# Half of the query turns and half of the context turns as two-byte DMA transposes in a two-layer transformer kernel

## The chip, the cores and the metric

The kernel runs on one core of a Trainium2 chip. The core has five engines, each with an instruction queue of its own that is worked off in order: TensorE (matrix products, named PE in the profile; PEld is its weight load), VectorE (DVE), ScalarE (ACT), GpSimd (POOL) and SyncE (SP), which only issues DMAs. Sixteen DMA engines move the data of all queues. The metric is the device time of one execution in microseconds. Before the change it is 1984.88 us, the median of three runs (1981.24 to 1986.15).

## The reference

Two layers work on x of shape (4, 512, 512): four sequences of 512 tokens with 512 features. Each layer adds an attention and a mixture of experts to x, both taken from the same layer norm. The change lies in the attention of the first layer, which in short is

```python
xn = layernorm(x)
q  = rope(rmsnorm(xn @ Wq))              # 16 heads of 128
lk = rope(rmsnorm(xn @ Wlk)); lv = xn @ Wlv
# a compressed memory: every 4 tokens make one entry, keys ck and values cv
sc = q @ ck.T * scale                    # causal, the 8 largest per query are kept
ctx_sparse = softmax(top8(sc)) @ cv
# a local window: 128 tokens back
ctx_local = softmax(mask(q @ lk.T * scale)) @ lv
out = concat_heads((ctx_sparse + ctx_local) * 0.5) @ Wo
x = x + out + moe(xn)                    # 8 experts, the 2 best per token
```

The second layer (plain attention with 16 heads of 32 and a second mixture of experts) is not touched.

## The kernel before, in words

**Steps.** The first layer's attention is a loop over 32 steps. A step is a pair (g, b): a group g of two heads (there are eight) and a sequence b (four). Step i computes the attention of its two heads, while the projections of step i+1 are computed between its parts. `project(i + 1)` returns the pieces of the next step, which the loop calls at chosen places: `first`, `second`, `third`, `fourth` and `fifth` compute queries, keys and values of 512 tokens by seven block products in place of eight (L750 to L802). The queries come out with tokens on the partitions, in two tiles `qb[0]` (tokens 0 to 255) and `qb[1]` (256 to 511).

**Turns.** The scores need queries with features on the partitions, so each half is turned: `turn_queries(t)` (L737) makes four 128x128 transposes on TensorE into one bank of PSUM (tile `trq`), and ScalarE copies the bank into `qkT` (L742). The keys are turned in the same way by `turn_keys` (L744). `qkT` has one buffer, shared by the step at work and the next.

**Attention of one head.** `scores` (L807) makes compressed scores (tile `sp`, L820) and local ones (`st`, L831); `turn` (L859) turns the chosen weights into `sT`, with two ScalarE copies; `context` (L870) multiplies by the values (L881 to L886), and ScalarE and VectorE scale and add both parts into a tile of tag `ctx` (L897, L899). This tag has two buffers. `turn_context(i, h, ...)` (L903) turns the 512x128 contexts of a head by four transposes on TensorE (tile `trc`) and a ScalarE copy into `cT` (L907), one tile with one buffer for both heads.

**Output.** In steps 5 to 23 `output7` (L932) multiplies `cT` by Wo with seven block products; its `before` part needs only the first 256 tokens of head 0 (the product x, tile `ox`, L945). In the other steps `output` (L909) makes four products over both heads (`op`, L914).

**What else lies in the steps.** `run0((i, h))` calls the jobs listed for a place of a step. From step 5 to step 22 these are the experts of the first layer, two tiles of 128 tokens per step: `apply` (L545, the products `hp_r` at L552, the sum `yr_r` at L555, its store `yd` at L561), the fetch of the weights by GpSimd (L489), and the tokens of later tiles. These tokens already come by transfer: they lie in DRAM split into low and high two-byte halves, GpSimd gathers them (L524), SyncE stores them (L529, `xrd_r`), and a DMA transpose loads them turned (L534, `xT_r`), one half-step ahead of their use. From step 24 on the expert outputs are gathered and added, and from step 29 the next layer's layer norm begins, with its stores on SyncE (L250, L1125).

**What sets the order.** The framework plans the kernel ahead of its execution: each instruction goes to its engine's queue in an order that follows the text of the program, corrected by estimated times, and waits by semaphores on what it reads or overwrites. A tile that reuses a buffer waits until all users of the buffer's last tile are done. Instructions wrapped in `tc.keep_in_program_order` keep the order of the text among each other; the rest may be moved. The DMAs of SyncE stand in one queue: `L685` loads sums of the inputs for the next step, `L1271` copies 32 rows of compressed values for a later step, L561 stores expert outputs.

Of the kernel before, what the change touches and what calls it, by code (L numbers as in the profile page):

```python
# [12 lines left out]
F32 = mybir.dt.float32  # L13
# [7 lines left out]
P = 128  # L21
# [3 lines left out]
TC = S // P  # L25
KC = HID // P
NH, D = 16, 128
# [9 lines left out]
HG = 2  # L37
# [9 lines left out]
U16 = mybir.dt.uint16  # L47
# [3 lines left out]
def two_layers(ctx: ExitStack, tc: tile.TileContext, a: dict, out: bass.AP, large: bass.AP):  # L51
# [3 lines left out]
    nc = tc.nc  # L55
    V, G, A, PE = nc.vector, nc.gpsimd, nc.scalar, nc.tensor
# [4 lines left out]
    dram = ctx.enter_context(tc.tile_pool(reuse_waits="tile", name="dram", bufs=1, space=DRAM))  # L61
# [6 lines left out]
    wk0 = layer0.enter_context(tc.tile_pool(reuse_waits="tile", name="att0", bufs=2))  # L68
# [5 lines left out]
    def psum(tag, name):  # L74
        return ps.tile([P, 512], F32, tag=tag, name=name, bufs={"mm": 3, "sc": 3, "tr": 2}[tag])
# [22 lines left out]
    def load_later(g):  # L98

        w = load_block(g, "wB")  # L100
        b2 = wpool.tile([P, 2, 3 * D], F32, tag="b2", name=f"b2_{g}")
        for i, nm in enumerate(("bA", "bB")):
            nc.sync.dma_start(out=b2[:, i, :], in_=a[nm][g].partition_broadcast(P))
        return [[None, w], b2]

    def load_out(g):
        wo = wpool.tile([P, HG, HID], F32, tag="Wo", name=f"Wo_{g}", bufs=1)
        nc.sync.dma_start(out=wo, in_=a["Wo"][ds(g * HG * D, HG * D), :].rearrange("(h p) c -> p h c", p=P))
        return wo
# [357 lines left out]
    class Experts:  # L467
# [58 lines left out]
        def store_halves(self, i):  # L526
            if i < NS:
                xd = self.xd[i] = dram.tile([P, 2, HID], U16, tag="xrd", name=f"xrd_{self.r.name}_{i}", bufs=3)
                tc.keep_in_program_order(nc.sync.dma_start(out=xd.rearrange("p h d -> p (h d)"), in_=self.x.pop(i)))  # L529
# [6 lines left out]
        def turn(self, i):  # L536
            x = self.x[i]
            tr = self.bank("tr", f"trm_{self.r.name}_{i}")
            for k in range(KC):
                PE.transpose(tr[:, ts(k, P)], x[:, ts(k, P)], ident)  # L540
            xT = self.pool.tile([P, KC, P], F32, tag="xT", name=f"xT_{self.r.name}_{i}", bufs=2 if self.silu else 1)
            A.copy(xT, tr.rearrange("p (k t) -> p k t", k=KC))
            self.x[i] = xT
# [136 lines left out]
    def load_sums(i):  # L680

        for n in range(4):
            xs[n] = wk0.tile([P, 2, 256], F32, tag=f"x{n}", name=f"x{n}_{i}", bufs=1)
            if i >= B:
                nc.sync.dma_start(out=xs[n].rearrange("p k t -> p (k t)"), in_=xsd[steps[i][1], n])  # L685

    def project(i):


# [3 lines left out]
        qkT = qp.tile([P, 2 * HG, S], F32, tag="qkT", name=f"qkT_{g}_{b}", bufs=1)  # L693
        x11, x12, x21, x22 = (xnT[:, ts(f, 2), ds(b * S + t * 256, 256)] for t in range(2) for f in range(2))
        rows3 = [P, 2, 3 * D]
        u, qb, sq = {}, {}, {}
# [40 lines left out]
        def turn_queries(t):  # L737
            tr = psum("tr", f"trq_{i}_{t}")
            for h in range(HG):
                for c in range(2):  # L740
                    PE.transpose(tr[:, ts(h * 2 + c, P)], qb[t][:, c, ts(h, D)], ident)  # L741
            A.copy(qkT[:, 0:HG, ts(t, 256)], tr.rearrange("p (h t) -> p h t", h=HG))  # L742

        def turn_keys(h):  # L744
            tr = psum("tr", f"trk_{i}_{h}")
            for t in range(TC):
                PE.transpose(tr[:, ts(t, P)], lv[:, t, 2, 0:D] if h else qb[t // 2][:, t % 2, ts(2, D)], ident)  # L747
            A.activation(qkT[:, HG + h, :], tr, AF.Copy, scale=turned[:, 0:1])
# [121 lines left out]
    def context(i, h, lT, sT, lv):  # L870

        g, b = steps[i]
        nm = f"{g}_{b}_{h}"
        U = D + 1

        ca, cb, cc = (psum("sc", f"c{x}_{nm}") for x in "abc")
        loc = [ca[:, ts(t, U)] if t < 3 else cb[:, 0:U] for t in range(TC)]
        spa = [cc[:, 0:U], cc[:, ts(1, U)], cb[:, ts(1, U)], cb[:, ts(2, U)]]
        for t in range(TC):
            if t:  # L880
                PE.matmul(loc[t], lhsT=lT[:, ds((t - 1) * 256 + P, P)], rhs=lv[:, t - 1, h, :],  # L881
                          start=True, stop=False)
            PE.matmul(loc[t], lhsT=lT[:, ds(t * 256, P)], rhs=lv[:, t, h, :],  # L883
                      start=(t == 0), stop=True)
        for t, at, n in ((2, 0, 96), (3, 1, P), (0, 0, P), (1, 2, P)):
            PE.matmul(spa[t], lhsT=sT[0:n, ts(at, P)], rhs=cv[0:n, b, :] if t else cv0s[i % 2],  # L886
                      start=True, stop=True)
        sums = small.tile([P, 8], F32, tag="sums", name=f"sums_{nm}")
        for dst, bank, n in ((0, ca, 3), (3, cb, 3), (6, cc, 2)):
            V.tensor_scalar(sums[:, ds(dst, n)],  # L890
                            bank[:, 0 : n * U].rearrange("p (n u) -> p n u", u=U)[:, :, D],
                            1e-30, None, ALU.max)
        V.reciprocal(sums, sums)
        ctx_ = wk0.tile([P, TC, D], F32, tag="ctx", name=f"ctx_{nm}")
        for t in (2, 3, 0, 1):
            at = (6, 7, 4, 5)[t]
            A.activation(ctx_[:, t, :], spa[t][:, 0:D], AF.Copy, scale=sums[:, at : at + 1])  # L897
        for t in range(TC):
            V.scalar_tensor_tensor(ctx_[:, t, :], loc[t][:, 0:D], sums[:, t : t + 1], ctx_[:, t, :],  # L899
                                   ALU.mult, ALU.add)  # L900
        return ctx_

    def turn_context(i, h, ctx_, cT):  # L903
        tr = psum("tr", f"trc_{i}_{h}")
        for t in range(TC):
            PE.transpose(tr[:, ts(t, P)], ctx_[:, t, :], ident)
        A.copy(cT[:, h, :], tr)  # L907
# [125 lines left out]
    for b in range(1, B):  # L1033
        i = b - 2
# [118 lines left out]
    for n in range(3 * TC):  # L1153
        i, t = 29 + n // TC, n % TC
# [22 lines left out]
    qkT, sums_x, first, second, third, fourth, fifth, turn_queries, turn_keys, sevenths = project(0)  # L1177
# [83 lines left out]
    for i, (g, b) in enumerate(steps):  # L1261
        if b == 0:
            if g:
                out_w[g] = load_out(g)
            if g + 1 < NH // HG:
                groups[g + 1] = load_later(g + 1)
        more = i + 1 < len(steps)
        turn_last = turn_keys
        now = qkT
        cT = qp.tile([P, HG, S], F32, tag="cT", name=f"cT_{g}_{b}", bufs=1)  # L1270
        nc.sync.dma_start(out=cv0s[i % 2][96:P, 0:D], in_=cv[0:32, b, 0:D])  # L1271
        em0, lT0 = scores(i, 0, now, (lambda: (turn_last(1), next(comp[0]))) if i == 0 else None)
        if i:
            turn_last(1)
        if more:
            load_sums(i + 1)
            qkT, sums_x, first, second, third, fourth, fifth, turn_queries, turn_keys, _ = project(i + 1)
            first()
            sums_x()
            if b == 2 and g + 1 in groups:  # L1280
                groups[g + 1][0][0] = load_block(g + 1, "wA")
        run0((i, 0))
        em1, lT1 = scores(i, 1, now)
        if i == 0:
            second(0)
        sT0 = turn(i, 0, em0)
        run0((i, 1))
        if more:
            if i:
                second(0)  # L1290
            if i != 3:
                turn_queries(0)
        ctx0 = context(i, 0, lT0, sT0, lv)
        if more:
            if i == 3:
                turn_queries(0)
            second(1)
        sT1 = turn(i, 1, em1)
        if more:
            third()  # L1300
        if b == 2 and g + 1 in groups:
            combine_weights(g + 1)
        run0((i, 2))
        ctx1 = context(i, 1, lT1, sT1, lv)
        turn_context(i, 0, ctx0, cT)
        if i == 5 or b == 0 and 5 < i < 24:
            combine_out(g)
        run0((i, 3))
        if more:
            fourth()  # L1310


            if 5 <= i < 24:
                turn_queries(1)
                turn_keys(0)
                fifth()
            else:
                fifth()
        seven = 5 <= i < 24
        if seven:  # L1320
            before, rest_ = output7(i, cT)
            before()
        turn_context(i, 1, ctx1, cT)
        if more and not 5 <= i < 24:
            turn_queries(1)
            turn_keys(0)
        run0((i, 3.5))
        if seven:
            rest_()
        else:  # L1330
            for t in range(TC):
                output(i, t, cT)
        run0((i, 4))
# [240 lines left out]
    order1, whole_, halves_ = [], list(range(FULL)), list(range(FULL, NS))  # L1574
# [875 lines left out]
```

## Time and profile before

| | us |
|---|---|
| median of three runs | 1984.88 |
| the profiled execution | 1984.9 |
| its span, first to last instruction | 1983.1 |
| a step with experts (6 to 18) | 44.0 |
| a step after the experts (24 to 28) | 38.0 |
| mean of one transpose as listed, L741 and L906 | 0.276 |
| ScalarE copy behind it, L742 and L907 | 0.587 and 0.577 |

The granted TensorE clock is 0.997 over the span. A line of the groups or of the timeline gives the line of the kernel, the engine, the operation, the tiles (written<-read) with shape and type, and the count; the timeline begins with start and length in us, both merged over the count. Matmuls are pipelined, so lengths of neighbours overlap, and the time that one takes from TensorE is read from the distance of starts. In the waits, a line names who waited, for whom, the total in us, the number of waits and the longest. In the windows each engine has its busy time and instruction count; PEclk is the granted clock, DMA the busy share of the sixteen DMA engines.

### The profile page before, as it was taken

The page shows a single profiled execution, that of the slowest core. Times are in us where ns is not written, and L with a number is a line of the kernel's source. Part 1 is how long each engine was busy: PE and PEld are TensorE (multiplying, and loading weights), DVE is VectorE, ACT ScalarE, POOL GpSimd, SP SyncE. Part 2 cuts the span into 40 slices and gives each one's busy share as a digit, 9 for nine tenths or more (in the row PEclk, how much of TensorE's full clock was granted, in tenths as well). Part 3 has the DMA queues.
Part 4 walks back from the last instruction along what each step waited for, and adds up shares of the span by engine and source line. Part 5 has one row for each costly group of instructions (what it writes and reads, how often), then busy time and mean ns, then how long its engine had stood idle before and what let it go on. Part 6 is the DMA issues. An engine that isn't in the chain of part 4 may idle for free.

```text
span 1983.1 us, 28429 instructions
## 1 busy us (share of the span) xinstructions
PE 1953.7 (99%) x9222; PEld 1228.8 (62%) x9222; DVE 1481.3 (75%) x3662; ACT 870.8 (44%) x2650; POOL 755.7 (38%) x827
## 2 busy tenths in 40 slices
PE   7999999999999999999999999999999999999998
PEld 4676667777777677776667776666434445445443
DVE  7778878777776777777678888788696655666886
ACT  5556544444444444444444455445234433333342
POOL 5422254443423333334432454455114432333551
PEclk9999999999999999999999999999999999999999
DMA  9224355544554464356572322232317775775441
GB/s 298 97 69 134 128 162 161 165 134 130 159 157 134 139 183 139 112 163 191 192 223 57 97 75 65 86 96 75 119 44 265 254 255 186 276 251 177 156 157 63
DMA packets 147294, 298.74 MB, mean 151 GB/s; under 512 B 53568, under 2 KB 67008, under 8 KB 135360
## 3 DMA queue, kind: packets, MB, share of 16 engines
q1 hardware_dynamic: 118912, 145.81, 24.0%
q0 software_dynamic: 27072, 148.91, 22.6%
q10 hardware_dynamic: 1152, 2.10, 0.3%
q8 instruction: 76, 1.25, 0.3%
q14 instruction: 82, 0.67, 0.1%
HBM read 230.44 MB, written 56.36 MB: 145 GB/s over the span
## 4 chain that ended last, share of the span: by engine, by line
PE 85%; DVE 9%; ACT 3%; issue 1%; DMA 1%; POOL 0%; SPq 0%; DVEq 0%; ACTq 0%; POOLq 0%
PE p L717 24%; PE hp_r L552 13%; PE op L914 4%; PE st L831 4%; PE st L1483 3%; PE po L1621 3%; PE cx L1497 3%; PE qp L1459 3%; PE sp L820 3%; PE ox L945 2%; PE o L1566 2%; PE ca L883 2%; PE oz L945 1%; PE trk L747 1%; PE trq L741 1%
## 5 line engine op out<-in xcount | busy, mean ns | idle before, releaser
L552 PE MATMUL hp_r<-we_r,xT_r 128*128 128x512 f32 (+1 forms) x592 | 224.2, 596 | 0.8 <-DVE qk L1472 0.8
L606 POOL TENSOR_TENSOR ss_q<-ss_q,nhalf 128x4 f32<-128x4 f32 x64 | 71.1, 1111 | 366.1 <-ACT ss_q L603 366.1
L839 POOL TENSOR_TENSOR lT<-lT,lmask 128x512 f32<-128x512 f32 (+1 forms) x128 | 150.2, 1187 | 105.8 <-ACT lT L835 104.8
L717 PE MATMUL p<-wT,x 128*128 128x384 f32 x512 | 176.6, 488 | 1.5 <-DVE wT L121 1.1
L717 PE MATMUL p<-wB,x 128*128 128x384 f32 x512 | 177.0, 490 | 0.1
L717 PE MATMUL p<-wA,xnT 128*128 128x384 f32 x512 | 173.6, 490 | 0.4 <-DVE u L757 0.3
L835 ACT ACTIVATE lT<-st,ss_k 128x256 f32<-128x256 f32 (+1 forms) x256 | 98.9, 441 | 161.1 <-PE st L831 159.4
L1485 ACT ACTIVATE pT<-st 128x1024 f32<-128x1024 f32 x128 | 123.3, 1016 | 59.0 <-PE st L1483 43.7
L552 PEld LDWEIGHTS hp_r<-we_r,xT_r 128*128 128x128 f32 (+1 forms) x592 | 83.2, 170 | 96.2 <-issue 93.4
L717 PEld LDWEIGHTS p<-wB,x 128*128 128x128 f32 x512 | 94.2, 191 | 63.1 <-issue 7.3
L717 PEld LDWEIGHTS p<-wT,x 128*128 128x128 f32 x512 | 93.4, 190 | 63.8 <-issue 4.8
L717 PEld LDWEIGHTS p<-wA,xnT 128*128 128x128 f32 x512 | 95.0, 192 | 60.4 <-DVE u L757 2.9
L601 ACT ACTIVATE sq_q<-qb 128x128 f32<-128x128 f32 x256 | 79.2, 310 | 117.1 <-DVE qb L763 54.9
L831 PE MATMUL st<-qkT 128*128 128x256 f32 (+1 forms) x512 | 114.6, 353 | 0.0
L569 POOL DMA_INDIRECT row_r<-yd,slot_r x64 | 72.1, 1127 | 75.0 <-issue 28.7
L831 PEld LDWEIGHTS st<-qkT 128*128 128x128 f32 x512 | 92.2, 190 | 11.5 <-issue 1.8
L914 PE MATMUL op<-Wo,cT 128*128 128x512 f32 x208 | 92.8, 593 | 0.0
L735 ACT ACTIVATE qb<-qb,ss_q 128x128 f32<-128x128 f32 x256 | 81.8, 392 | 21.3 <-POOL ss_k L605 16.0
L606 POOL TENSOR_TENSOR ss_k<-ss_k,nhalf 128x2 f32<-128x2 f32 (+1 forms) x96 | 86.7, 903 | 8.0
L742 ACT COPY qkT<-trq 128x512 f32<-128x512 f32 x64 | 37.6, 587 | 118.0 <-PE trq L741 78.8
L717 PE MATMUL p<-wT,xnT 128*128 128x384 f32 x256 | 88.1, 487 | 0.3 <-DVE wT L121 0.3
L605 POOL TENSOR_SCALAR ss_k<-ss_k 128x2 f32<-128x2 f32 (+1 forms) x96 | 35.0, 364 | 137.4 <-ACT sq_k L601 131.2
(388 smaller groups left out, 4598.1 us busy)
## 6 DMA issues: line engine op xcount, KB each, us to landing
x<-xsd SPq DMA_DIRECT2D x112, 256.0 KB
yd<-yr_r SPq DMA_DIRECT2D x72, 256.0 KB
xrd_r<-xr_r SPq DMA_DIRECT2D x36, 256.0 KB
wA<-in_wA SPq DMA_DIRECT2D x16, 384.0 KB
wB<-in_wB SPq DMA_DIRECT2D x16, 384.0 KB
xnd<-xn SPq DMA_DIRECT2D x24, 256.0 KB
accd<-acc SPq DMA_DIRECT2D x18, 256.0 KB
acc<-in_x SPq DMA_DIRECT2D x16, 256.0 KB
```

The costliest lines, as they stand in the source:

```text
L552: PE.matmul(hp[ts(h, m), :], lhsT=xT[:, k, ts(h, m)], rhs=w[:, ts(k, HID)], start=(k == 0), stop=(k == KC - 1))
L569: G.indirect_dma_start(out=x, out_offset=None, in_=self.yd, in_offset=at_rows(self.r.slot[:, k, n : n + 1]))
L601: pin(A.activation(sq, x[:, h, :], AF.Square, accum_out=ss[:, j : j + 1]))
L606: pin(G.tensor_tensor(ss, ss, nhalf[:, 0:n], ALU.pow))
L717: fixed(PE.matmul(p, lhsT=x[:, k, ts(c, P)], rhs=w[:, k, :], start=(k == 0), stop=(k == 1)))
L735: A.activation(x[:, j, :], x[:, j, :], AF.Copy, scale=scale[:, n : n + 1])
L820: PE.matmul(sp[:, seen[t]], lhsT=qkT[:, h, ts(t, P)], rhs=ckT[:, b, 0 : 32 * (t + 1)], start=True, stop=True)
L831: PE.matmul(st[:, ds((t % 2) * 256, n)], lhsT=qkT[:, HG + h, ts(t, P)], rhs=qkT[:, h, ds(t * P, n)], start=True, stop=True)
L835: A.activation(lT[:, ds(half * 512 + c * 256, n)], st[:, ds(c * 256, n)], AF.Exp, scale=norm_k[(i, h)][2 * half + c])
L839: G.tensor_tensor(dst, dst, lmask.rearrange("p a w j -> p (a w j)")[:, 0:n], ALU.mult)
L914: PE.matmul(op, lhsT=cT[:, h, ts(t, P)], rhs=wo[:, h, :], start=(h == 0), stop=(h == HG - 1))
L1485: A.activation(pt[:, ts(pair, 2), :], st, AF.Exp, scale=SCALE1)
```

## The change

From step 5 on the first 256 queries of the next step, and the contexts of head 0 of every step, are no longer turned by TensorE. ScalarE copies the tile into a buffer of tag `ctx`, splitting each four-byte number into its two two-byte halves, so that low halves and high halves lie in separate runs. SyncE stores the result in DRAM and loads it back by a DMA transpose of two-byte elements, which writes the halves of a number next to each other, so that the target tile, read as four-byte numbers, holds the turned matrix. Both sides move 256 KB. The split of the queries stands where `turn_queries(0)` stood; their store stands after the first head's `context`; the load after the second head's `turn`. The split of the contexts stands right behind `context(i, 0)`, their store behind `turn(i, 1)`, their load after the jobs of place 2. Stores and loads keep the order of the text. The second half of the queries, the keys, and the contexts of head 1 are turned as before, and so are the queries of the steps up to 5 and the contexts of the steps up to 4.

```diff
@@ -684,6 +684,23 @@
             if i >= B:
                 nc.sync.dma_start(out=xs[n].rearrange("p k t -> p (k t)"), in_=xsd[steps[i][1], n])
 
+    by_transfer = {}
+
+    def split_halves(nm, x):
+        h = wk0.tile([P, TC, D], F32, tag="ctx", name=f"halves_{nm}")
+        h = h.bitcast(U16).rearrange("p n f -> p (n f)").rearrange("p (c x f) -> p c x f", c=x.shape[1], x=2)
+        A.copy(h, x)
+        return h
+
+    def store_halves(nm, h):
+        c, f = h.shape[1], h.shape[3]
+        xd = dram.tile([c, P, 2, f], U16, tag=f"halves{c}", name=f"halvesd_{nm}", bufs=2)
+        tc.keep_in_program_order(nc.sync.dma_start(out=xd.rearrange("c p x f -> p c x f"), in_=h))
+        return xd
+
+    def load_halves(out, xd):
+        tc.keep_in_program_order(nc.sync.dma_start_transpose(out=out, in_=xd.rearrange("c p x f -> (c p x) f")))
+
     def project(i):
 
 
@@ -740,6 +757,14 @@
                 for c in range(2):
                     PE.transpose(tr[:, ts(h * 2 + c, P)], qb[t][:, c, ts(h, D)], ident)
             A.copy(qkT[:, 0:HG, ts(t, 256)], tr.rearrange("p (h t) -> p h t", h=HG))
+
+        def split_queries():
+            return split_halves(f"q_{i}", qb[0][:, :, 0 : 2 * D].bitcast(U16).rearrange("p c (f x) -> p c x f", x=2))
+
+        def load_queries(xd):
+            load_halves(qkT[:, 0:HG, 0:256].bitcast(U16), xd)
+
+        by_transfer[i] = split_queries, load_queries
 
         def turn_keys(h):
             tr = psum("tr", f"trk_{i}_{h}")
@@ -1288,21 +1313,35 @@
         if more:
             if i:
                 second(0)
-            if i != 3:
+            if i >= 5:
+                split_q, load_q = by_transfer.pop(i + 1)
+                halves_q = split_q()
+            elif i != 3:
                 turn_queries(0)
         ctx0 = context(i, 0, lT0, sT0, lv)
+        if i >= 5:
+            halves_c = split_halves(f"c_{i}", ctx0.bitcast(U16).rearrange("p n (f x) -> p n x f", x=2))
+            if more:
+                halves_q = store_halves(f"q_{i}", halves_q)
         if more:
             if i == 3:
                 turn_queries(0)
             second(1)
         sT1 = turn(i, 1, em1)
+        if i >= 5:
+            halves_c = store_halves(f"c_{i}", halves_c)
+            if more:
+                load_q(halves_q)
         if more:
             third()
         if b == 2 and g + 1 in groups:
             combine_weights(g + 1)
         run0((i, 2))
+        if i >= 5:
+            load_halves(cT[:, 0:1, :].bitcast(U16), halves_c)
         ctx1 = context(i, 1, lT1, sT1, lv)
-        turn_context(i, 0, ctx0, cT)
+        if i < 5:
+            turn_context(i, 0, ctx0, cT)
         if i == 5 or b == 0 and 5 < i < 24:
             combine_out(g)
         run0((i, 3))
```

## The prediction

> **What bounds the kernel now.** I read the page's busy shares and chain first, then the windows, the waits of TensorE, and the order of one step on TensorE, SyncE and ScalarE.
>
> ```profile
> span 1983.1 us, 28429 instructions
> PE 1953.7 (99%) x9222; PEld 1228.8 (62%) x9222; DVE 1481.3 (75%) x3662; ACT 870.8 (44%) x2650; POOL 755.7 (38%) x827
> PE 85%; DVE 9%; ACT 3%; issue 1%; DMA 1%; POOL 0%; SPq 0%; DVEq 0%; ACTq 0%; POOLq 0%
> ```
>
> TensorE is busy 99% of the span and carries 85% of the chain that ended last. The windows of one expert step (step 9, from its first scores to the next step's) and of one later step (step 24) show that nothing else is near it:
>
> ```profile
> core 0: us, PE busy (x) PEld busy (x) DVE busy (x) ACT busy (x) POOL busy (x), PEclk, DMA share, GB/s
> 434.43:478.43 44.00, 44.00 (x209) 31.49 (x208) 31.27 (x88) 19.23 (x71) 14.72 (x16) 1.00 0.49 145
> 1097.00:1135.00 38.00, 38.00 (x176) 26.22 (x175) 29.15 (x81) 19.11 (x70) 15.19 (x17) 1.00 0.35 112
> ```
>
> TensorE has no gap in either; VectorE is free for 12.7 of 44 us and for 8.9 of 38. In the waits of TensorE between 260 and 1395 us no line waits more than 1.0 us in all. So a slot that leaves TensorE shortens the step, as long as nothing new makes TensorE wait. This is the order on TensorE, the stretch that the change touches:
>
> ```profile
> 456.38 0.60 PE L741 MATMUL trq<-ident,qb 128*128 128x128 f32 x4
> 456.81 0.39 PE L883 MATMUL ca<-lv,lT 128*128 128x129 f32 x2
> 466.32 0.61 PE L886 MATMUL cb<-cv,sT 96*128 96x129 f32 x4
> 467.22 0.60 PE L906 MATMUL trc<-ident,ctx 128*128 128x128 f32 x4
> 467.65 3.60 PE L552 MATMUL hp_r<-we_r,xT_r 128*128 128x512 f32 x8
> 477.13 1.03 PE L945 MATMUL ox<-Wo,cT 128*128 128x256 f32 x4
> 478.43 0.81 PE L820 MATMUL sp<-ckT,qkT 128*128 128x32 f32 x6
> ```
>
> The first column is the start. The reader should take starts, not durations: 456.38 to 456.81 and 467.22 to 467.65, so four turns hold TensorE 0.43 to 0.44 us, though each is listed with 273 ns. The last two lines are the first users of what will come by transfer: the first head's contexts at 477.13, the next step's queries at 478.43. SyncE's queue in the same stretch:
>
> ```profile
> 456.43 0.34 SPq L529 DMA_DIRECT2D xrd_r<-xr_r  x1
> 458.51 1.59 SPq L534 DMA_TRANSPOSE xT_r<-xrd_r  x1
> 460.76 1.62 SPq L685 DMA_DIRECT2D x<-xsd  x2
> 467.19 0.53 SPq L1271 DMA_DIRECT2D cv<-cv  x1
> 472.01 0.33 SPq L561 DMA_DIRECT2D yd<-yr_r  x1
> 472.45 0.36 SPq L529 DMA_DIRECT2D xrd_r<-xr_r  x1
> ```
>
> It is nearly empty, but it runs in order, and several entries stand there waiting for their data.
>
> **What is removed.** Steps 5 to 30 lose one turn of queries (26), steps 5 to 31 one turn of contexts (27): 53 groups of four transposes. At 0.435 us of TensorE a group this is 53 x 0.435 = 23.1 us, 0.87 us in a step that loses both. Their 53 ScalarE copies out of PSUM go too (L742 587 ns, L907 577 ns).
>
> The Trainium skill, "Perfetto Trace Analysis", section Identifying the Most-Contended Engine, calls matmul busy time a bad measure and wants the share of weight loads, here 62%; priced by weight loads (212 of 141 ns) the removed part would be 29.9 us and the sum 6.8 us lower. The trace sides with the starts: the matmuls follow each other without a gap, and a turn frees only its 109 ns.
>
> **What is added on ScalarE.** 53 copies of 128x1024 two-byte elements. The same form is in the trace, for the expert rows:
>
> ```profile
> L1062 ACT COPY xh<-xw x16: 1028/1048/1077, 182.2 to 213.5; 128x1024 uint16<-128x1024 uint16 x16
> ```
>
> 53 x 1.05 = 55.6 us, less 30.9 us of copies that go: 24.7 us more on an engine that is busy 19.2 of 44 us, so 0.9 us a step beside TensorE. Uncovered, this would cost those 24.7 us; what covers it is ScalarE's idle time (2.4 us waiting for sums at 457 to 460, 1.3 at 461).
>
> **What is added on SyncE and the DMA engines.** 53 stores to DRAM and 53 turning loads, of 256 KB each. The expert rows already take this path twice a step. From the trace's records of landings, the store L529 lands 2.3 us after its start (median; 1.9 to 9.3), the turning load L534 5.9 us (3.2 to 10.1), and the latter holds the queue 1.4 us (1.2 to 4.1). The long ones lie beside the weight fetches of GpSimd's queue (128 packets of 10 KB each). Shapes differ (512x256 and 1024x128 halves in place of 256x512), the bytes and the 256-byte packets do not; I take the medians and keep the ends. 27 MB more, on DMA engines busy about half the time, has room.
>
> **The contexts' path in step 9.** The queries are scaled at 452.8; ScalarE can split them by 455. Their store is held behind the expert store in written order: 456.8, landed at 459.1 (to 466.1). The first head's context is merged at 461.75. Its halves take the buffer that the queries' halves held (three tiles now go through two buffers before the second head's context), so the copy waits for that landing: by the median none, copy 461.8 to 462.9. Store at 463.0, landed 465.3. SyncE meanwhile issues the queries' load and, now behind it, the expert load L534, 1.4 us each: 463.4 to 466.2. Context load from 466.2, landed at 472.1 (469.4 to 476.3). Product x wants it at 476.7 (477.13 less the group that leaves in front of it): 4.6 us spare, 0.4 at the load's worst, late by about 10 only if all three transfers take their worst. The queries' load, from 463.4, lands at 469.3 (to 473.5), wanted at 477.6: 4 us spare at worst.
>
> What moves back in the queue has time: the expert load (issued 6 us later than now) serves a product in the next step, at 494; the x loads and the cv copy serve the next step too. The waiting copy blocks ScalarE, and behind it stand the copies of sT (L866, 462.38), which TensorE's L886 wants at 466.32.
>
> Steps 24 to 31 have less: context merged at 1115.9, wanted at 1127.4. Copy 1.1, store 0.1 + 2.3, load 5.9 give 1125.3, 2.1 us spare at the median, up to 9 late if both transfers are at their worst; with the DMA engines at 0.35 instead of 0.49 I take the median. In step 31 there are 8.8 us between merge and use (1383.3 to 1392.1) against 9.4: some 0.6 us late.
>
> Sum: 1984.9 (the profiled execution's own time: its span of 1983.1 and 1.8 around it; the median of the three runs is 1984.88, the same) - 23.1 + 0.6 = 1962.4.
>
> **Rivals.**
>
> *Half eaten.* In four to seven of the nine steps from 23 on both transfers run at the third quartile (store 4.7, load 7.9: 2.3 us late each), or the ScalarE hold below comes in every second expert step (9 x 1.3 us): 9 to 16 us back, 1972 to 1979. For it: the spare time of 2.1 us is small. Against: the lighter traffic there.
>
> *ScalarE held.* The copy of the context's halves is planned before the copies of sT and waits for the queries' store. If that lands at its worst, 466.1 (beside the weight fetch that GpSimd issues at 456.16), copy 1.05 and sT 0.37 end at 467.6, 1.3 us after L886 wants it. Over 18 expert steps 23.4 us: 1985, no change. For it: the fetch does start there. Against: the expert store that leaves 0.4 us ahead (456.43) landed after 2.0 us in this step and in most others.
>
> *Context load behind the expert's store (slower).* The order on SyncE is the planner's; if it puts the context load behind L561, which stands until 471.98 for its data, the load starts at 472.4, in the middle of the weight fetch issued at 472.25. At the third quartile (7.9) it lands at 480.3, 3.6 us after product x wants it, and TensorE stands: 18 x 3.6 = 65 us, so 2027 (1991 at the median 5.9, 2066 at 10.1). It decides from 1.28 us a step (23.1/18). For it: in the waits of the queue, this line stands longest.
>
> ```profile
> SPq L561 <- DVE yr_r L555: 303.5, 36, 19.1
> SPq L534 <- DMA xrd_r<-xr_r: 55.1, 22, 7.0
> ```
>
> Against: the load is written before that expert's product, and its store has landed some 7 us earlier. The Trainium skill, "VectorE: DVE Perf Modes", Rules for kernel authors, sides with this rival: it would turn 128x128 blocks on TensorE wherever PSUM will do as the target. The trace agrees on the latency (some 9 us for copy, store and load against 0.44 + 0.58), and says nothing against hiding it.
>
> *TensorE is not what is freed.* The slots go but VectorE or a PSUM bank then paces the step: with 12.7 us free on VectorE I give it no share of its own; it is in the middle cases.
>
> **How the numbers follow.** Forecast 0.48 (1960 to 1968); half eaten 0.12; ScalarE held, or a mixture that lands within 0.3% (6 us, about what can be told from no change), 0.10; context load late 0.30. So faster 0.60, same 0.10, slower 0.30. The range reaches from 1958 (sum without any lateness, 1961.8, less the 3.6 us by which the lowest run before lies under the median) to 2000: above it lies about half of the last rival, below it 0.03.
>
> **What will show it.** Right: no trq of the first half and no trc of head 0 after step 5, steps of 43.1 us, and no wait of TensorE for a DMA. ScalarE held: TensorE's L886 waits for sT, ScalarE's split copy for a store. Load late: TensorE's product x or output waits for the DMA into cT; queries late: the first scores wait for the DMA into qkT. Wrong would be a plan in which the consumers were moved ahead of the landings, or turning loads of these shapes that take more than 10 us.

## The result and the profile after

The changed kernel takes 1978.95 us (median; 1974.01 to 1985.39), the kernel before beside it 1984.28 (1980.46 to 1987.02): 5.3 us less, ratio 0.9976 with a 95% interval of 0.9967 to 0.9984. That lies within the 0.3% named above as about what can be told from no change; with twenty runs of each kernel the interval still leaves no change out. 1962.4 was forecast, so the sign is right and three quarters of the 22.5 us are missing. The profiled execution took 1975.01 us, the second-shortest of the twenty, so some 4 us of what the median lost stand in no trace. The page of the kernel after:

```profile
span 1973.2 us, 28229 instructions
PE 1933.4 (98%) x9010; PEld 1206.8 (61%) x9010; DVE 1481.5 (75%) x3662; ACT 892.8 (45%) x2650; POOL 756.1 (38%) x827
...
PE 79%; DVE 10%; DMA 4%; ACT 3%; issue 2%; POOL 1%; SPq 0%; DVEq 0%; ACTq 0%; POOLq 0%
...
halvesd_c<-halves_c SPq DMA_DIRECT2D x27, 256.0 KB, 3.5
halvesd_q<-halves_q SPq DMA_DIRECT2D x26, 256.0 KB, 2.9
```

TensorE has 212 matmuls less, as it should (53 groups of four). But its share of the chain fell from 85% to 79%, and transfers rose from 1% to 4%: there is a new wait. Windows of the kernel after, each from a step's first scores to the next's: steps 9, 8, 24 and 20, in this order.

```profile
core 0: us, PE busy (x) PEld busy (x) DVE busy (x) ACT busy (x) POOL busy (x), PEclk, DMA share, GB/s
432.45:477.10 44.65, 43.38 (x201) 30.72 (x199) 30.99 (x88) 19.95 (x71) 14.71 (x16) 1.00 0.57 165
389.33:432.45 43.12, 43.12 (x201) 30.66 (x199) 33.49 (x92) 19.94 (x71) 20.97 (x21) 1.00 0.56 163
1090.18:1127.25 37.07, 37.07 (x167) 25.25 (x167) 30.03 (x82) 20.17 (x70) 15.34 (x17) 1.00 0.49 143
910.81:956.65 45.84, 44.07 (x216) 29.88 (x215) 32.62 (x92) 19.94 (x71) 18.18 (x20) 1.00 0.64 207
```

Step 8 went from 44.0 to 43.12, step 24 from 38.0 to 37.07, with no gap on TensorE: 0.88 us each, the forecast's 0.87. Steps 9 and 20, though, have 1.3 and 1.8 us in which TensorE stands. By the distances from one step's turn of its chosen weights to the next step's, step 9 is 0.66 us longer than before, steps 19, 20, 21 and 22 are 0.98, 1.16, 1.56 and 0.38 longer, 29 and 30 1.92 and 0.81; most others are 0.88 shorter. In all, steps 5 to 18 are 11.1 us shorter, steps 19 to 22 4.1 longer and steps 23 to 30 2.2 shorter, where 0.87 a step would have been 12.2, 3.5 and 7.0 us shorter. The waits of TensorE in the kernel after, from 260 to 1395 us:

```profile
engine line waited for: us in total, times, longest us
PE cb L911 <- ACT sT L891: 6.0, 4, 2.2
PE trx L255 <- DVE xn L247: 3.6, 1, 3.6
PE p L734 <- DVE u L800: 1.5, 1, 1.5
```

Before, no line had more than 1.0. The first is the rival *ScalarE held*. Step 9 shows it. TensorE in the kernel after (start, length, instruction):

```profile
463.68 0.39 PE L908 MATMUL cb<-lv,lT 128*128 128x129 f32 x2
465.33 0.71 PE L911 MATMUL cb<-cv,sT 96*128 96x129 f32 x4 [1.27 <-ACT sT L891]
...
475.80 1.03 PE L970 MATMUL ox<-Wo,cT 128*128 128x256 f32 x4
```

ScalarE there:

```profile
451.86 1.04 ACT L692 COPY halves_q<-qb 128x1024 uint16<-128x1024 uint16 x1
...
463.96 1.04 ACT L692 COPY halves_c<-ctx 128x1024 uint16<-128x1024 uint16 x1 [5.28 <-DMA halvesd_q<-halves_q]
464.92 0.36 ACT L891 COPY sT<-trs 128x256 f32<-128x256 f32 x1
```

and SyncE:

```profile
454.08 0.34 SPq L529 DMA_DIRECT2D xrd_r<-xr_r  x1
454.52 0.94 SPq L698 DMA_DIRECT2D halvesd_q<-halves_q  x1
458.33 1.61 SPq L685 DMA_DIRECT2D x<-xsd  x2
465.03 0.39 SPq L698 DMA_DIRECT2D halvesd_c<-halves_c  x1
465.52 1.30 SPq L702 DMA_TRANSPOSE qkT<-halvesd_q  x1
466.91 1.25 SPq L534 DMA_TRANSPOSE xT_r<-xrd_r  x1
468.26 1.25 SPq L702 DMA_TRANSPOSE cT<-halvesd_c  x1
```

The order on SyncE is the forecast's, queries' load, expert load, contexts' load. But the queries' store, issued at 454.52, lands at 463.9, 9.3 us later; the contexts are merged at 459.3, and their copy stands on ScalarE until the store has released its buffer. Behind it stands the copy of sT, and TensorE waits for that. The context load itself landed 0.4 to 7.1 us ahead of its use in every step of this profile. From each transfer's records of landings, in us:

| step | queries' store lands after | contexts merged | their copy starts | TensorE waits for sT |
|---|---|---|---|---|
| 5 to 8 | 2.4 | | within 0.1 | 0 |
| 9 | 9.3 | 459.3 | 464.0 | 1.3 |
| 10 to 19 | 2.5 to 4.1 | | within 0.1 | 0 |
| 20 | 9.6 | 938.0 | 943.2 | 1.8 |
| 21 | 9.8 | 983.9 | 989.4 | 2.2 |
| 22 | 9.1 | 1030.1 | 1034.3 | 0.8 |

Step 19 has no such wait; there TensorE's expert product (L552) waits 0.8 us for a weight fetch, which landed 11.6 us after its issue (the same fetch before the change: 9.6).

The late store of step 9 is no accident of this execution: in the nine profiles here in which both queries and contexts of this step go by transfer, it lands after 7.4 to 9.4 us, and the store of step 18 after 2.8 to 9.6.

The second wait, 3.6 us in step 29, is the same buffer by another way: the queries are split at 1291.1, but their store leaves SyncE only at 1296.9, behind stores of the next layer's norm that wait there; it lands at 1300.4, the contexts' copy starts at 1300.5, and the squares behind it (L601) reach VectorE late, which then is late with xn (L247). The third, 1.5 us, lies in step 30 and is taken up further down.

In SyncE's own waits, in the kernel after, the expert store still stands longest, 261.0 us for 303.5; the expert load, now behind other entries, waits 27.4 itself where it waited 55.1:

```profile
SPq L561 <- DVE yr_r L555: 261.0, 36, 19.0
```

### The profile page after: what moved, and what is told of

It reads as the page before. It is cut to its first block, busy times and chain, and to the rows that moved or that the text cites. A ratio compares the mean times of both kernels' runs of the same rounds, so it can differ in the third digit from the quotient of the medians.

```text
span 1973.2 us, 28229 instructions
## 1 busy us (share of the span) xinstructions
PE 1933.4 (98%) x9010; PEld 1206.8 (61%) x9010; DVE 1481.5 (75%) x3662; ACT 892.8 (45%) x2650; POOL 756.1 (38%) x827
## 4 chain that ended last, share of the span: by engine, by line
PE 79%; DVE 10%; DMA 4%; ACT 3%; issue 2%; POOL 1%; SPq 0%; DVEq 0%; ACTq 0%; POOLq 0%
PE p L734 23%; PE hp_r L552 12%; PE op L939 4%; PE st L856 4%; PE st L1522 3%; PE po L1660 3%; PE cx L1536 3%; PE qp L1498 3%; PE sp L845 2%; PE ox L970 2%; PE o L1605 2%; DMA halvesd_q<-halves_q 2%; PE oz L970 1%; PE ca L908 1%; PE trk L772 1%
## 5 line engine op out<-in xcount | busy, mean ns | idle before, releaser
L552 PE MATMUL hp_r<-we_r,xT_r 128*128 128x512 f32 (+1 forms) x592 | 226.4, 596 | 1.2 <-DMA we_r<-in_Wh,wrow_r 0.8
L552 PEld LDWEIGHTS hp_r<-we_r,xT_r 128*128 128x128 f32 (+1 forms) x592 | 83.6, 170 | 98.2 <-issue 92.8
L601 ACT ACTIVATE sq_q<-qb 128x128 f32<-128x128 f32 x256 | 79.2, 310 | 96.4 <-DVE qb L788 53.0
L569 POOL DMA_INDIRECT row_r<-yd,slot_r x64 | 72.5, 1133 | 74.5 <-DMA yd<-yr_r 21.8
L752 ACT ACTIVATE qb<-qb,ss_q 128x128 f32<-128x128 f32 x256 | 81.8, 392 | 21.3 <-POOL ss_k L605 16.0
L489 POOL DMA_INDIRECT xr_r<-xnd,rows_r x36 | 40.5, 1125 | 120.6 <-PE trm_r L540 88.4
L922 ACT ACTIVATE ctx<-cb,sums 128x128 f32<-128x128 f32 x128 | 39.7, 360 | 101.0 <-DVE sums L918 93.6
```

The source lines that it names most:

```text
L552: PE.matmul(hp[ts(h, m), :], lhsT=xT[:, k, ts(h, m)], rhs=w[:, ts(k, HID)], start=(k == 0), stop=(k == KC - 1))
L569: G.indirect_dma_start(out=x, out_offset=None, in_=self.yd, in_offset=at_rows(self.r.slot[:, k, n : n + 1]))
L601: pin(A.activation(sq, x[:, h, :], AF.Square, accum_out=ss[:, j : j + 1]))
L752: A.activation(x[:, j, :], x[:, j, :], AF.Copy, scale=scale[:, n : n + 1])
```

## Experiments

All kernels compute the whole reference. "Less" is the median of the kernel before, run beside it, minus its own; the changed kernel's is 5.3.

**Another buffer for the queries' halves.** They are put into the half of the context tile cT that is free at that time, so that the contexts' halves find a free ctx buffer. The orders on all five queues are unchanged.

```diff
-                halves_q = split_q()
+                halves_q = split_q(cT[:, 0, :])
```

> The only edit: the queries' halves lie in the idle first half of cT instead of a tile of tag ctx; all five queues keep their order. Theory (ScalarE is held by the shared buffer: the split of the contexts waits until the store of the queries has landed, and the copies of sT and the squares stand behind it): no wait of ScalarE for halvesd_q, no wait of TensorE for sT, steps 9 and 20 to 22 back at 43.1 to 43.9 us, step 29 at about 40 to 41; 1962 to 1967 us. Rival 1 (the added traffic itself slows the weight fetches and the other loads, and TensorE waits for those): 1977 to 1981, as changed. Rival 2 (TensorE's clock is granted less): 1977 to 1981 with a lower granted clock.

Measured: 1971.56 (1963.16 to 1984.81), 12.3 less, ratio 0.995 (0.9921 to 0.9978). In the profiled execution (1966.33) no wait for sT is left, step 9 takes 43.12, steps 20 to 22 take 43.8, although the queries' store of step 9 still lands after 9.4 us and those of steps 20 to 22 after 9.1 to 9.7. So the hold is real: the same late stores cost nothing where nothing waits for their buffer. Step 19 stays at 46.16 us (44.69 before); there the expert product waits for the weight fetch, which lands after 12.1 us (9.6 in the kernel before), so rival 1 holds in this one step:

```profile
PE hp_r L552 <- DMA we_r<-in_Wh,wrow_r: 1.3, 1, 1.3
```

The median is above the 1962 to 1967 of the theory, and the runs now spread over 22 us, against 6.5 of the kernel before beside them.

**Each part alone.** The queries alone go by transfer, then the contexts alone; the other turns stay on TensorE.

```diff
-        if i >= 5:
-            halves_c = split_halves(f"c_{i}", ...)
...
-        if i < 5:
-            turn_context(i, 0, ctx0, cT)
+        turn_context(i, 0, ctx0, cT)
```

> Only the queries go by transfer; the contexts of head 0 are turned by TensorE as before. No third tile in tag ctx between queries and contexts, so nothing waits for the queries' store but their own load. Theory: 26 x 0.435 = 11.3 us less than before, 1972 to 1975. Rival 1 (traffic): half of the change's gain, 1980 to 1983. Rival 2 (clock): the same, 1980 to 1983.

```diff
-            if i >= 5:
-                split_q, load_q = by_transfer.pop(i + 1)
-                halves_q = split_q()
-            elif i != 3:
+            if i != 3:
                 turn_queries(0)
```

> Only the contexts of head 0 go by transfer; the queries are turned by TensorE as before. The split of the contexts now waits for no store of queries. Theory: 27 x 0.435 = 11.7 us less than before, 1972 to 1975. Rival 1 (traffic): 1980 to 1983. Rival 2 (clock): 1980 to 1983.

Measured: queries alone 1975.06 (1974.15 to 1977.9), 8.8 less, ratio 0.9952 (0.9939 to 0.9964); contexts alone 1972.95 (1971.23 to 1975.28), 10.9 less, ratio 0.9942 (0.9929 to 0.9955). At 0.435 a group 11.3 and 11.7 were due, and both intervals hold them. With the contexts alone most steps are exactly 0.44 us shorter, 43.56 for 44.0. So each part delivers about its price, 19.7 us together, and what is missing comes of their being together. The late stores alone do not: with the queries alone the stores of steps 20 and 21 land after 10.0 and 11.0 us, and these steps are still 0.44 us shorter.

**The hold taken off sT.** The shared buffer stays, but the contexts' split stands behind the two copies of sT, in written order.

```diff
         sT1 = turn(i, 1, em1)
         if i >= 5:
+            halves_c = split_halves(f"c_{i}", ...)
             halves_c = store_halves(f"c_{i}", halves_c)
```

> The shared buffer stays; the split of the contexts is put behind the two copies of sT of the second head on ScalarE, and this order is fixed. Nothing else moves. Theory: TensorE no longer waits for sT (6.0 us in the profile of the changed kernel), but the squares of the next queries still stand behind the held split, so steps 29 and 30 keep their loss: 1970 to 1976. Rival 1 and 2: 1977 to 1981.

Measured: 1972.13 (1971.87 to 1977.5), 11.8 less, ratio 0.9943 (0.9931 to 0.9955). Its waits of TensorE:

```profile
PE p L736 <- DVE yr_r L555: 4.3, 3, 2.3
PE trx L255 <- DVE xn L247: 4.3, 1, 4.3
```

The wait for sT is gone, and a wait for VectorE stands in its place: what is now behind the held copy on ScalarE is squares that VectorE needs. An engine that stands holds whatever is next, so in this execution reordering moved the wait. It is one of the two longer executions, though (1976.67; four of the six took 1972.0 us, give or take 0.3). At the median the new order won back about as much as the other buffer, 11.8 us less against 12.3; no trace shows how long TensorE waits in the shorter executions.

**Steps 19 to 22 without transfers.** In these steps an expert tile needs two fetches of weight rows (L489, two tables in place of one), and in the changed kernel's profile all long stores of queries but step 9's lie here. Three variants: the version with the halves in cT, without transfers in these steps; the same with transfers only in these; and the changed kernel, shared buffer kept, without transfers in them.

```diff
+    on = lambda i: i >= 5 and not 19 <= i < 23
...
-        if i >= 5:
+        if on(i):
```

> As e1 (queries' halves in cT), but the transfers are left out in steps 19 to 22, where the expert tiles need two weight fetches each and TensorE turns as before: 22 + 23 = 45 groups, 19.6 us. Theory A (the runs of e1 spread from 1963 to 1985 because in steps 19 to 22 the added traffic meets the doubled weight fetches): the spread goes, 1963 to 1968. Theory B (the spread comes from elsewhere, such as steps 29 to 31 or the clock at the start): the spread stays at 15 us or more, median 1968 to 1975.

> As e1, but the transfers are used in steps 19 to 22 alone: 8 groups, 3.5 us to win. Theory A: single runs lose far more than that, median 1979 to 1986 with a spread of 10 us or more. Theory B: 1979 to 1982 with the spread of before (7 us).

> The changed kernel with its shared buffer, without the transfers in steps 19 to 22 (19.6 us to win). If the held ScalarE costs what the profile of the changed kernel shows outside these steps (1.3 us in step 9, 3.6 in step 29, 1.5 to 2.5 in step 30): 1968 to 1973. If the shared buffer costs nothing there, as e5: 1963 to 1968.

Measured: without them 1967.69 (1966.97 to 1968.41), 17.9 less, ratio 0.9912 (0.9899 to 0.9925); only in them 1985.5 (1980.48 to 1994.05), ratio 1.0003 (0.9988 to 1.0017); shared buffer without them 1974.22 (1972.19 to 1978.86), 11.4 less, ratio 0.9947 (0.9933 to 0.9961). Two things follow. At the median the four steps lose all that their eight groups should gain (3.5 us), and they make the spread: 1.4 us without them, 13.6 with them alone. They do not lose in every execution: in the profile of the kernel with them alone (1984.57) these steps are 2.9 us shorter than before, no wait of TensorE from 260 to 1395 us is over 1.0, and 2.7 us are lost ahead of step 5, where the two kernels are the same. And the shared buffer costs 6.5 us (1974.22, a little above the 1968 to 1973 expected, against 1967.69) in the other steps: beside the version without the buffer, steps 9, 18 and 29 of the profiles are 0.7, 1.4 and 3.0 us longer. Step 22 is 0.7 longer too, without a transfer in it, so this part is not shown to be the buffer's.

**A long execution of the version with the halves in cT.** The first variant was run again, beside these.

> e1 once more, for a second profile and more times. Theory of the first experiments (the shared buffer costs what the change lost): median 1964 to 1972, below the changed kernel's 1979 in most runs. Theory A: slow runs again, and in a profile of one TensorE waits for weights or for the sum of an expert tile in steps 19 to 22. Theory B: its waits lie elsewhere.

Measured: 1973.22 (1963.97 to 1986.77), 12.4 less, ratio 0.9934 (0.9914 to 0.9954). The profile happened to catch a long execution, 1984.28 us, in which step 20 takes 62.08 us and the others are as in the first profile. TensorE there:

```profile
950.68 2.75 PE L735 MATMUL p<-wB,x 128*128 128x384 f32 x8
969.05 2.05 PE L971 MATMUL ox<-Wo,cT 128*128 128x256 f32 x4 [15.63 <-DMA cT<-halvesd_c]
```

SyncE and then GpSimd of the same execution:

```profile
944.46 1.24 SPq L703 DMA_TRANSPOSE qkT<-halvesd_q  x1
945.79 1.25 SPq L534 DMA_TRANSPOSE xT_r<-xrd_r  x1
947.14 2.57 SPq L703 DMA_TRANSPOSE cT<-halvesd_c  x1
```

```profile
947.20 0.94 POOL L489 DMA_INDIRECT we_r<-in_Wex,wrow_r  x1 [1.15 <-PE hp_r L552]
948.45 0.94 POOL L489 DMA_INDIRECT we_r<-in_Wh,wrow_r  x1 [0.30 <-issue]
```

The product x waits 15.6 us for the contexts' load, which landed 21.8 us after its issue. It left 0.06 us ahead of the next tile's weight fetches. The load of the queries, 2.7 us ahead of them, landed after 3.6. The place is that of theory A, the steps 19 to 22; what is waited for is neither the weights nor the sum that it named.

**One transfer at a time in steps 19 to 22.** The halves are in cT; in these four steps only the contexts, or only the queries, go by transfer.

```diff
-    on = lambda i: i >= 5 and not 19 <= i < 23
+    on_q = lambda i: i >= 5 and not 19 <= i < 23
+    on_c = lambda i: i >= 5
```

> The queries' halves lie in the context tile cT everywhere; in steps 19 to 22 only the contexts go by transfer, the queries are turned on TensorE. Theory (the queue of SyncE): in the step that lost 15.6 us, the load of the contexts was issued at 947.1 because the load of the queries stood in front of it, waiting from 938.8 to 944.4 for the late store of the queries; so it met the weight fetches issued from 947.2 on. Without the queries, the load of the contexts is issued some 4 us or more ahead of those fetches and is in time: four steps gain 0.44 us each, so 1.7 us under the version without transfers in these steps (1967.7 beside a before of 1985.6), some 1966, and no run more than 3 us above the median. Rival (the load itself is slow in these steps, wherever it stands): the product x still waits in some runs, the median is 1968 to 1971 and single runs lie 5 us or more above the lowest.

> As the run with the contexts alone, but in steps 19 to 22 only the queries go by transfer and the contexts are turned on TensorE. Theory (the queue of SyncE): nothing of the contexts stands behind the late store; the load of the queries, issued at 944.5 at worst, has until the next step's first scores, so again 1.7 us under 1967.7, some 1966, without spread. A small loss is possible where the copy of the turned contexts into cT waits for the late store that reads the halves there (the copy stands some 10 us behind the split, so 0 to 1 us a step). Rival (each turning load in these steps is caught by itself): the first scores of a step wait for the transfer into qkT in some runs, median 1968 to 1971, spread of 5 us or more.

Measured: contexts alone 1967.02 (1965.5 to 1970.45), 19.6 less, ratio 0.9906 (0.989 to 0.9923); queries alone 1967.4 (1966.26 to 1967.67), 19.3 less, ratio 0.9902 (0.9885 to 0.9919). Both are about 1 us above the 1966 expected, and one run of the contexts' lies 3.4 above its median where 3 was the limit. Still each is clean: steps 19 to 21 take 44.25 where all on TensorE they take 44.68. So a turning load in these steps is not slow by itself. Steps 29 and 30, though, gain nothing in both versions: with the contexts alone in steps 19 to 22 these two take 40.75 and 37.86 us (40.88 and 37.06 before), and TensorE's waits from 260 to 1395 us begin with three in them:

```profile
PE trx L255 <- DVE xn L247: 1.5, 1, 1.5
PE p L735 <- DVE u L801: 1.5, 1, 1.5
PE p L735 <- DVE u L815: 1.0, 1, 1.0
```

All three are for VectorE, which works on the next layer's layer norm there as well and in step 30 is busy 36.05 of the 37.86 us. In the run with the contexts alone everywhere the two steps had gained 0.7 and 0.4 us, so it is the queries' part that brings nothing there; why, no run shows. That the cause of the late loads is the queue of SyncE was not yet shown: with one transfer there is less traffic too.

**The order of the loads turned round.** All transfers in all steps, halves in cT, but the queries' load is written behind the contexts'.

```diff
         sT1 = turn(i, 1, em1)
         if i >= 5:
             halves_c = store_halves(f"c_{i}", halves_c)
-            if more:
-                load_q(halves_q)
...
             load_halves(cT[:, 0:1, :].bitcast(U16), halves_c)
+            if more:
+                load_q(halves_q)
```

> As the version with the queries' halves in the context tile, all transfers in all steps; only the order of the turning loads on SyncE is changed: expert load, contexts' load, queries' load in place of queries, expert, contexts. Theory (the queue of SyncE): the contexts' load no longer stands behind the queries' load, which waits for the late store; it is issued one or two turning loads (1.3 to 2.7 us) earlier where it mattered, product x is served in time in steps 19 to 22, and the median falls from some 1972 to 1966 (before 1984 to 1986), with runs within 3 us. Rival (the traffic of both): in step 20 the contexts' own store lands 7 to 8 us after its issue, against 5.5 us where the contexts go alone, so their load cannot start before 946.7 whatever the order on SyncE; it meets the weight fetches of 947 as before, the median stays at 1970 to 1974 and single runs reach 1979 or more.

Measured: 2004.9 (1994.36 to 2017.99), 21 us slower than the kernel before, ratio 1.012 (1.0095 to 1.0144). Neither theory said that, though the rival's premise held: the contexts' own stores landed after 6.5 to 7.8 us. SyncE, GpSimd, ScalarE and TensorE in step 21 of this kernel:

```profile
1001.34 1.78 SPq L703 DMA_TRANSPOSE cT<-halvesd_c  x1
1003.17 1.29 SPq L703 DMA_TRANSPOSE qkT<-halvesd_q  x1
```

```profile
1003.24 0.94 POOL L489 DMA_INDIRECT we_r<-in_Wex,wrow_r  x1 [1.15 <-PE hp_r L552]
```

```profile
1020.38 0.59 ACT L760 COPY qkT<-trq 128x512 f32<-128x512 f32 x1 [17.97 <-DMA qkT<-halvesd_q]
```

```profile
1009.05 1.03 PE L971 MATMUL ox<-Wo,cT 128*128 128x256 f32 x4
1021.02 1.12 PE L932 MATMUL trc<-ident,ctx 128*128 128x128 f32 x4 [10.94 <-ACT qkT L760]
```

The contexts' load is in time now, and the queries' load, last in the queue, has its place beside the fetch. It lands 17.1 us after its issue; ScalarE's copy of the other queries into the same tile waits 18 us for it, its bank of PSUM is not freed, and TensorE stands 10.9 us. The theory of the queue was right that the order on SyncE decides which load is late, and wrong that a load ahead of the other would cure it: now the last one leaves beside the fetch and is caught. The last turning load of the steps in question, in five profiles (us; the fetch's issue after the load's, negative where it was ahead):

| kernel, step | fetch after load | load lands after |
|---|---|---|
| changed kernel, 19, 20, 21 | 0.90, 2.75, 2.66 | 3.4, 3.1, 3.1 |
| halves in cT, 19, 20, 21 | 1.05, 1.31, 1.30 | 3.3, 5.3, 5.1 |
| the same, long execution, 19, 20, 21 | 0.91, 0.06, 1.38 | 3.3, 21.8, 5.7 |
| contexts alone, 19, 20, 21 | 1.83, 2.17, 3.11 | at least 3.9, 3.8, 4.7 (not every part's landing is on record) |
| order turned round, 19, 20, 21 | -0.24, -0.75, 0.08 | 12.0, 11.3, 17.1 |

From 0.9 us ahead of the double fetch on, these loads land in 3 to 6 us (in the kernel with transfers in steps 19 to 22 alone, 0.7 and 0.8 ahead, in 4.6 and 4.1); 0.1 us ahead of it or behind it, in 11 to 22. The contexts' loads of the kernel with the order turned round, 0.5 to 1.9 us ahead, landed in 3.4 to 7.1, so the edge lies between 0.1 and 0.5; it is not sharp, since the expert load of the long execution, 1.4 us ahead, took 9.0. A load that meets a double fetch still on its way is slow too: the queries' load of step 19, issued 5.8 us behind the second fetch of the tile before, took 9.0 us in the changed kernel. The version with the halves in cT mostly has 0.9 to 1.4 us to spare in these steps, so its long execution was decided by a margin of about one microsecond. The changed kernel's own profile has 2.7 us in steps 20 and 21, presumably because the hold delays TensorE, and the fetch follows TensorE's products (in the long execution it waited 1.15 us for one); in step 19, without the hold, it has 0.9.

## Why the prediction was off

**What is removed: right.** 0.88 us in a step that loses both turns, 0.44 in a step that loses one. The rival price by weight loads (29.9 us for 53 groups, 0.56 each) is refuted by the same steps: the distance of starts was the right measure. The Trainium skill, "Perfetto Trace Analysis", section Identifying the Most-Contended Engine, asks for the share of weight loads, among other things, to judge how near TensorE is to its limit; it gives no price for a transpose that goes, and as a price the share does not hold here.

**What is added on ScalarE: right.** The copies take 1.04 to 1.05 us. ScalarE's busy time in step 8 is 19.9 us, and the step has no gap on TensorE: covered.

**What is added on SyncE and the DMA engines: the failed step.** "I take the medians and keep the ends": the stores do land in 2.1 to 4.1 us in most steps, and the contexts' load in 2.9 to 4.9. But the ends were not chance; they belong to certain steps. In steps 20 to 22 the queries' store, issued 0.8 to 1.8 us behind the first of two weight fetches, lands after 9.1 to 9.8. The median over all steps hid that four steps have twice the weight traffic, and the trace of the kernel before showed it: its three slowest expert stores (7.9, 9.3 and 8.8 us, at 913.7, 958.8 and 1003.4) lie in steps 19, 20 and 21. For steps 9 and 18, with single fetches, the runs show that the store is late and not why.

**The contexts' path: "by the median none" failed with it.** The merge came at 459.3, 2.4 us earlier than written because the steps ahead are shorter, and the order on SyncE is the forecast's; the 4.6 us spare of the context load was 4.3. But in step 9 itself, the one worked out, the queries' store landed after 9.3 (0.35 us behind a single fetch, which in steps 10 to 18 of this profile cost nothing like it), so the copy that was to wait "by the median none" waited 4.6 us and TensorE 1.3. The rival *ScalarE held* had the right place and a good price (1.3 us a step; 1.3, 1.8, 2.2 and 0.8 measured) and the wrong number of steps: four of 18, and step 29 by the squares. Its argument against, that the expert store 0.4 us ahead lands in 2.0 us, was read from a step with a single fetch, in which the stores 0.3 to 0.5 us behind a fetch mostly do land in 2.5 to 4.

**The steps after the experts: better than forecast, but for one.** Steps 24 to 28 have 2.8 to 5.8 us spare where 2.1 were worked out, and step 31 1.7 in place of 0.6 late. Step 29 was not seen: SyncE's queue holds the queries' store itself, 5.8 us, behind stores of the next layer. The forecast looked at what is queued behind a waiting transfer, not at what the new store queues behind there. And with any buffer steps 29 and 30 gain nothing once the queries go by transfer, and TensorE waits 4.0 us for VectorE in them. This is what the rival *TensorE is not what is freed* describes; it had no share of its own on the strength of the 12.7 us that VectorE has free in step 9, which these two steps do not have.

The rule of the Trainium skill, "VectorE: DVE Perf Modes", Rules for kernel authors, to turn such blocks on TensorE, is right for steps 19 to 22 when both go by transfer, and wrong for most others, where the hidden transfers gain 0.44 us a group of four.

***Context load behind the expert's store*: refuted as stated,** since the load stands ahead of L561 in the queue. But product x waiting for a load that meets a weight fetch is what the long execution of the version with the halves in cT shows, by a margin, not by the order. *Half eaten* was nearest in time (1972 to 1979), by the hold, in its second form, and not by spare time lost after step 23; that the time fell into its bounds is in part luck, since step 19 lost by a slow fetch and step 29 by a queued store, which it did not name.

**The sum.** Of 22.5 us, 5.3 came. Without transfers in steps 19 to 22 the kernel gains 11.4, so there they lose 6.1 net; with another buffer besides 17.9, so the hold costs 6.5 in the other steps; with the contexts back in the four steps 19.6. These are differences of medians, each known to some 3 us. This last version removes 49 groups, 49 x 0.435 = 21.3 us, and its interval (0.989 to 0.9923 of 1986.66: 15.3 to 21.9 us) holds that sum. What is left open: why the stores of steps 9 and 18 are late, and whether the longer executions of the changed kernel itself (to 1985) are the same meeting of load and fetch; none of them was profiled.

## What to carry to other kernels

A transfer's landing time should be read step by step, beside what else the DMA engines carry then, before a median is put into a sum; here the slow tail was a place. Ask of every new transfer which buffer it holds, which in-order engine waits for that buffer, and what stands behind the waiting instruction: a store that is off the path can stop TensorE through a copy on ScalarE. And where two changes each gain their price alone and little together, look for the thing that they share, here a buffer and one stretch of the DMA engines.

## What was not expected of the hardware

**A turning load and a weight fetch that leave together slow each other far beyond their bytes.** The DMA view of the version with the halves in cT from 947 to 957 us, first in its first profile, where the contexts' load left 1.31 us ahead of the double fetch, then in the long execution, where it left 0.06 us ahead (packets and throughput, then for each queue its packets, MB and the time of the packets as a share of sixteen engines; q1 is SyncE's, q0 GpSimd's):

```profile
DMA packets 2635, 2.98 MB, mean 298 GB/s; under 512 B 2180, under 2 KB 2212, under 8 KB 2443
q0 software_dynamic: 286, 2.09, 63.8%
q1 hardware_dynamic: 2348, 0.88, 38.9%
```

```profile
DMA packets 2253, 1.20 MB, mean 120 GB/s; under 512 B 2145, under 2 KB 2145, under 8 KB 2209
q1 hardware_dynamic: 2126, 0.53, 94.9%
q0 software_dynamic: 126, 0.67, 30.4%
```

The same transfers stand there both times, and the engines are at least as busy, but they move well under half of the bytes per second. SyncE's queue takes 94.9% of sixteen engines for 0.53 MB, 0.07 us a packet in 10 us x 16; in the first profile it took 0.03. The load landed after 21.8 us and the two fetches after 22.2 and 24.0; in the first profile it was 5.3, 9.6 and 11.4. So it is not the overlap as such, which both executions have; what the traces show to differ is how close together they leave. The Trainium skill, "DMA: Bandwidth & Descriptors", section Queues, rings and completion order, says that a DMA engine goes round the queues that have work for it, a packet at a time. The trace agrees that both queues move in the same stretch; this rule alone gives no reason for the lower throughput, and no run here does.

**The clock after a stop.** In the long execution the granted clock falls to 0.50 while TensorE stands and stays there a little after; two windows of it:

```profile
957.00:969.00 12.00, 0.00 (x0) 0.00 (x0) 0.00 (x0) 0.00 (x0) 0.00 (x0) 0.50 0.97 149
956.60:973.70 17.10, 4.65 (x18) 4.19 (x19) 1.78 (x5) 0.89 (x3) 0.65 (x2) 0.51 0.91 185
```

The low stretch lasts 17.07 us, from 956.4 to 973.5, so 4.4 us of work after the stop ran at half the clock: step 20 was 18.3 us longer than in the first profile (62.08 against 43.81), 15.6 of it the wait and most of the rest slow matmuls (product x 2.05 us in place of 1.03). In the kernel with the split behind sT a wait of 2.3 us was followed by 3.41 us at half clock, and in the kernel with the order turned round the waits of 5.5, 5.8 and 10.9 us came with low stretches of 6.83, 6.83 and 13.65 us. So a stop of TensorE can cost more than its own length. In the changed kernel's profile it did not: no stop from 260 to 1395 us, the longest 3.6 us, brought a low stretch.
